# Withdrawing the order between different cells of one PSUM tile in a two-stream recurrence

## The chip, the cores and the metric

The kernel runs on one core of one Trainium2 chip. The metric is the device time of one execution in microseconds (us); the median of three runs stands for a kernel. The profile is of one further execution. Its engines are PE (matmul), DVE (vector), ACT (scalar and tables), POOL (GpSimd) and SP, whose queue issues all the DMAs named here. Each engine takes its own instructions strictly in the order in which the program lists them; between engines, and for data inside an engine, they wait on semaphores.

## What is computed

Two transformer-like layers over x of shape 16 x 512 x 256 (batch, time, channel). Layer 0 has a recurrent "fast weights" block and a low-rank GELU network; layer 1 has attention over a window of 64 with four global keys, and a channel mix. Only the recurrence matters here. For each of 16 x 16 pairs of batch and head it carries two small matrices, `W_in` and `W_out` (4 x 16 each), over 32 chunks of 16 tokens:

```python
def step(carry, xs):
    W_in, W_out = carry
    q_t, k_t, v_t, lr_t = xs
    k_h = softmax(einsum('blhd,bDhd->blhD', k_t, W_in)) * lr_t[..., 1:]
    q_h = softmax(einsum('blhd,bDhd->blhD', q_t, W_in))
    qk = einsum('bqhD,bkhD->bhqk', q_h, k_h) * mask
    o_t = einsum('bqhD,bDhd->bqhd', q_h, W_out) + einsum('bhqk,bkhd->bqhd', qk, v_t)
    W_out = W_out + einsum('bnhD,bnhd->bDhd', k_h, v_t)
    for _ in range(2):
        g_out = -attn(W_in, k_t, v_t)
        g_in = -attn(W_out, v_t, k_t)
        W_in = W_in - lr_in * g_in
        W_out = W_out - lr_out * g_out
    return (W_in, W_out), o_t
```

`attn` is a softmax of scores over the 16 tokens, times values. Every step needs the matrices of the one before it, so within one batch and head nothing of two chunks can run at once.

## The kernel before

The batch is cut into two halves of 8 (8 batches x 16 heads = 128 partitions), the time into 8 blocks of 64. A unit `u` is one half (`u % 2`) and one block (`u // 2`): 16 units. Each passes through five streams: `prepare` (projections, convolutions, loads and stores through DRAM), `chain` (the recurrence), `mlp` (output projection of the recurrence, low-rank network), `attend` (window attention) and `mix`. A timetable by hand gives each step of each stream a due time, and the steps are written down in that order. `chain(u)` lasts from u to u + 2, so at any time two chains run, one of each half: unit u in its first piece of 32 tokens and unit u - 1 in its second. A piece has two chunks. A chunk of unit 9 is called 9_0_1 below: unit, piece, chunk.

From the written order a scheduler makes the order on each engine: it takes instructions by their place in the written order, as their dependencies allow, on its own idea of durations.

The matrices and the small sums of both halves lie in one PSUM tile of one bank, `fw` (128 x 512, lines 493 to 508): the left 256 columns are the first half's, the right 256 the second's. `fast(half)` cuts out `w_in`, `w_out`, `w_outs` and the places of maxima and sums. Every instruction that reads or writes `fw` is DVE's. The framework orders any two uses of one PSUM tile of which one writes, whether or not they touch the same columns; so all the uses of `fw`, of both halves, stand on DVE in the order in which they were written.

One chunk, `recur` (line 585 on), by its lines:

- ACT copies k, q and v of the chunk into `tok` (L597). DVE multiplies `tok` by `w_in` and reduces (scores, L527 and L528): `sc_k`, `sc_q` into `scs`.
- `exp_tokens`: maximum (L539) and difference (L541) on DVE, exponential on ACT (L542, `e_k`). Then `hid` by L609, L612 and ACT's L613.
- `over_tokens` on DVE (L547, L548, L549: sum, reciprocal, scaling), then POOL's outer product `pd_o` (L534); L619 to L623 normalise `hid`, then POOL's `pd_kv` (L534).
- DVE adds `w_out` to `pd_kv` (L628), scans it (L631), copies its end to `fw` (L632), reduces `pd_o` (L636, `do`) and adds (L641).
- Scores of v (`sc_v`, `sv`), exponential `e_v`, `over_tokens` again, POOL's `pd_i` twice (L534); DVE reduces each (L636, `di`) and adds it to `w_in` (L649, L653).
- Scores `sk`, `e_k` again, POOL's second `pd_o`; its reduction and the addition to `w_out` (L657) are put off into the next chunk.
- POOL makes the output from the scan (L661 to L663) into the place of q.

At the end of a piece `finish_piece` normalises the output (L673 to L681; `ov` is L678 and L679) and stores it (L682); `load_piece` loads the next piece (L567, L569), for which the same buffers must be free, and normalises k and q (`ss_k`, `ss_q`: ACT's squares L558, DVE's sums L579, POOL's products L581). `finish_fast_weights` loads the output in another layout, `oT` (L693).

In `attend`, row pair r (0 to 3) of a unit finds its maxima (`sc` by PE, `mx` by DVE in L889 and L900, split by POOL in L215 and L217), then weighs (`pmx`, `st`, `py`, `pz` by PE; `pT` L926 and `rs` L978, L979 by ACT; `yT` L983 by DVE). Its keys are loaded by L790 into a buffer that the unit before has read.

The end of the kernel's main function runs the timetable:

```python
    for _, _, last, stream in sorted(steps, key=lambda s: s[:2]):
        next(stream, None)
        if last:
            assert next(stream, steps) is steps
```

Of the kernel before, what the change touches and what calls it, by code (L numbers as in the profile page):

```python
# [15 lines left out]
PSUM = bass.MemoryType.PSUM  # L16

P = 128
# [50 lines left out]
def parity_scales():  # L69

    ch = np.arange(P)
    even = (ch // D) % 2 == 0
    s = 1.0 / math.sqrt(D)
    group, slot = ch // 32, ch % 32
    part = slot // NS < NPART
    sel = -((slot[:, None] % NS == np.arange(NS)[None, :]) & part[:, None]).astype(np.float32)
    k2, pair, _ = np.unravel_index(np.arange(32), (2, 4, NGLOB))  # L80
    selg = np.stack(
        [(group[:, None] == pair) & (slot[:, None] % NS == 2 * k2 + e) & part[:, None] for e in range(2)], 1
    ).astype(np.float32)
    ones_g = np.tile(np.arange(8)[None, :] == (4 * k2 + pair)[:, None], (NR, 1))
    parts = [
        np.stack([even * s, ~even * s, even, ~even], 1),
        group[:, None] == np.arange(4)[None, :],
        sel,
        -selg.reshape(P, -1),
        ones_g,  # L90
    ]
    return np.ascontiguousarray(np.concatenate([p.astype(np.float32) for p in parts], 1))


@with_exitstack
def adaln_blocks(ctx: ExitStack, tc: tile.TileContext, a: dict, out: bass.AP):
# [11 lines left out]
    def ctile(shape, name):  # L108
        return const.tile(shape, F32, tag=name, name=name)
# [36 lines left out]
    for n in ("cq", "ck", "cv"):  # L146
        t = ctile([P, 2, 4], f"w_{n}")
# [345 lines left out]
    fw = ps_w.tile([P, 512], F32, tag="fw", name="fw")  # L493
# [637 lines left out]
    steps = []  # L1131
# [5 lines left out]
    for _, _, last, stream in sorted(steps, key=lambda s: s[:2]):  # L1137
        next(stream, None)
        if last:
            assert next(stream, steps) is steps  # L1140


# [52 lines left out]
```

## Time and profile before

| what | value |
|---|---|
| three runs | 3187.85, 3193.95, 3194.49 us; median 3193.95 us |
| span of the profiled execution, first to last instruction | 3186.8 us |
| mean granted clock of TensorE | 0.830 |
| first chunk of unit 0 begins | 118 us |
| first chunks of units 1, 4, 8, 12, 15 begin | 229, 704, 1403, 2136, 2679 us |
| last addition to `w_out` (L657) | 2876 us |
| `pwo` of the last unit begins (PE, output projection of its recurrence) | 2958 us |

The time of the profiled execution itself is not among the runs' times; its span lies 1.1 us under the fastest of them and 7.2 us under the median. A unit takes 171 to 177 us while units 4 to 7 begin, and 178 to 186 us from unit 8 to unit 13: attention over more than one block begins to cost there. Idle time is given per instruction with what ended it ("releaser").

### The profile page before, as it was taken

The page shows a single profiled execution, that of the slowest core. Times are in us where ns is not written, and L with a number is a line of the kernel's source. Part 1 is how long each engine was busy: PE and PEld are TensorE (multiplying, and loading weights), DVE is VectorE, ACT ScalarE, POOL GpSimd, SP SyncE. Part 2 cuts the span into 40 slices and gives each one's busy share as a digit, 9 for nine tenths or more (in the row PEclk, how much of TensorE's full clock was granted, in tenths as well). Part 3 has the DMA queues.
Part 4 walks back from the last instruction along what each step waited for, and adds up shares of the span by engine and source line. Part 5 has one row for each costly group of instructions (what it writes and reads, how often), then busy time and mean ns, then how long its engine had stood idle before and what let it go on. Part 6 is the DMA issues. An engine that isn't in the chain of part 4 may idle for free.

```text
span 3186.8 us, 47321 instructions
## 1 busy us (share of the span) xinstructions
PE 2368.4 (74%) x17232; PEld 1450.8 (46%) x17232; DVE 2392.2 (75%) x4513; ACT 1809.4 (57%) x3880; POOL 1588.0 (50%) x1447
## 2 busy tenths in 40 slices
PE   3540255868787887878787787878878788789996
PEld 2210123444444454555545455555545555455564
DVE  1678787878787887888887888888888878875221
ACT  1761364656666756566665656666565655455653
POOL 0245555556556555545546454554645465654111
PEclk7775686878797988879888888988888888889998
DMA  5420122132314131232304123230402312122011
GB/s 150 98 58 13 47 44 62 31 74 54 84 35 100 30 92 44 64 71 51 84 21 104 31 64 71 51 84 23 106 21 66 70 48 60 44 54 59 13 35 27
DMA packets 439307, 186.46 MB, mean 59 GB/s; under 512 B 323937, under 2 KB 413090, under 8 KB 439074
## 3 DMA queue, kind: packets, MB, share of 16 engines
q1 hardware_dynamic: 439074, 183.44, 23.6%
q8 instruction: 135, 2.21, 0.3%
q14 instruction: 98, 0.80, 0.1%
HBM read 116.66 MB, written 66.72 MB: 58 GB/s over the span
## 4 chain that ended last, share of the span: by engine, by line
DVE 36%; PE 21%; POOL 18%; ACT 12%; issue 8%; DMA 4%; SPq 1%; POOLq 0%; DVEq 0%; ACTq 0%
POOL pd_o L534 5%; DVE pd_kv L631 5%; POOL pd_i L534 4%; DVE sc_v L527 4%; DVE sv L528 3%; POOL pd_kv L534 3%; PE pproj L1005 2%; DVE do L636 2%; DVE di L636 2%; DVE mx L889 2%; DVE scs L528 2%; DVE sc_k L527 2%; PE ph L736 1%; DMA oT<-o 1%; POOL x L389 1%
## 5 line engine op out<-in xcount | busy, mean ns | idle before, releaser
L534 POOL TENSOR_TENSOR pd_o<-e_k,dt_v 128x1024 f32<-128x1024 f32 x128 | 299.4, 2347 | 206.8 <-DVE e_k L549 206.6
L534 POOL TENSOR_TENSOR pd_i<-e_v,dt_k 128x1024 f32<-128x1024 f32 x128 | 297.1, 2358 | 54.5 <-DVE e_v L549 54.5
L708 PE MATMUL pwo<-w_WoT,oT 128*128 128x256 f32 x256 | 106.3, 574 | 230.1 <-POOL oT L701 191.0
L873 PE MATMUL st<-qs,keys 32*128 32x128 f32 x2048 | 195.3, 329 | 75.4 <-DVE mx L889 37.2
L636 DVE TENSOR_REDUCE do<-pd_o 128x64 f32<-128x1024 f32 x126 | 152.5, 1214 | 123.2 <-POOL pd_o L534 123.2
L661 POOL TENSOR_TENSOR pd_kv<-hid,pd_kv 128x1024 f32<-128x1024 f32 x64 | 150.0, 2344 | 170.6 <-DVE fw L632 154.2
L873 PE MATMUL sc<-keys,qs 32*128 32x128 f32 x2048 | 183.4, 320 | 62.3 <-DVE mx L889 48.5
L873 PEld LDWEIGHTS st<-qs,keys 32*128 32x128 f32 x2048 | 165.7, 221 | 120.4 <-DVE mx L889 45.7
L636 DVE TENSOR_REDUCE di<-pd_i 128x64 f32<-128x1024 f32 x128 | 155.0, 1215 | 86.0 <-POOL pd_i L534 85.9
L873 PEld LDWEIGHTS sc<-keys,qs 32*128 32x128 f32 x2048 | 146.8, 210 | 129.1 <-DVE mx L889 68.1
L534 POOL TENSOR_TENSOR pd_kv<-hid,dt_v 128x1024 f32<-128x1024 f32 x64 | 151.6, 2368 | 84.2 <-DVE hid L623 76.4
L889 DVE TENSOR_REDUCE mx<-sc 128x4 f32<-128x512 f32 x256 | 168.9, 680 | 31.4 <-PE sc L870 31.3
L631 DVE TENSOR_TENSOR_SCAN pd_kv<-within,pd_kv 128x1024 f32<-128x1024 bf16 x64 | 186.4, 2912 | 0.8
L708 PEld LDWEIGHTS pwo<-w_WoT,oT 128*128 128x128 f32 x256 | 68.4, 287 | 258.3 <-POOL oT L701 205.7
L527 DVE TENSOR_TENSOR sc_k<-tok,fw 128x1024 f32<-128x1024 f32 x128 | 155.6, 1216 | 16.1 <-ACT tok L597 14.5
L926 ACT ACTIVATE pT<-st 128x512 f32<-128x512 f32 x256 | 134.3, 603 | 55.3 <-PE st L870 55.1
L224 ACT ACT_TABLE_LOAD x115 | 147.5, 1283 | 15.9 <-PE ph L736 10.0
L527 DVE TENSOR_TENSOR sc_v<-tok,fw 128x1024 f32<-128x1024 f32 x128 | 150.4, 1215 | 1.6
L528 DVE TENSOR_REDUCE sv<-sc_v 128x64 f32<-128x1024 f32 x128 | 149.6, 1209 | 0.0
L736 PE MATMUL ph<-PT,w_v 64*128 64x512 f32 x256 | 111.3, 685 | 36.1 <-ACT z L224 27.5
L1005 PE MATMUL pproj<-w_proj,yT 128*128 128x256 f32 x512 | 124.4, 387 | 11.5 <-DVE yT L983 9.7
L197 PE MATMUL pmx<-w_w_attnT,blocks 128*128 128x384 f32 x256 | 111.6, 563 | 7.9 <-DVE up_a L387 3.1
(251 smaller groups left out, 6730.5 us busy)
## 6 DMA issues: line engine op xcount, KB each, us to landing
values<-values SPq DMA_DIRECT2D x56, 256.0 KB
gate_a<-gates SPq DMA_DIRECT2D x64, 128.0 KB
xa<-in_x_dram SPq DMA_DIRECT2D x32, 256.0 KB
x<-in_x_dram SPq DMA_DIRECT2D x32, 256.0 KB
gate_c<-gates SPq DMA_DIRECT2D x64, 128.0 KB
gate_d<-gates SPq DMA_DIRECT2D x64, 128.0 KB
q<-y SPq DMA_DIRECT2D x64, 128.0 KB
dt_q<-q SPq DMA_DIRECT2D x32, 256.0 KB
```

The costliest lines, as they stand in the source:

```text
L224: ins = nc.scalar.activation(*args[0], **args[1])
L527: engine.tensor_tensor(pr, tok.unsqueeze(1).to_broadcast(every), w.unsqueeze(2).to_broadcast(every), mul)
L528: nc.vector.tensor_reduce(dst, pr, AX.X, add)
L534: engine.tensor_tensor(pr, hid.unsqueeze(2).to_broadcast(every), tok.unsqueeze(1).to_broadcast(every), mul)
L631: nc.vector.tensor_tensor_scan(flat, within, flat, 0.0, mul, add)
L636: nc.vector.tensor_reduce(t, pr, AX.X, add)
L661: nc.gpsimd.tensor_tensor(po, qh.unsqueeze(2).to_broadcast([P, R, D, CH]), upto, mul)
L708: nc.tensor.matmul(po[:, n * C : (n + 1) * C], lhsT=pair(oT, k, 2 * b2 + n), rhs=w_o[:, k, :], start=k == 0, stop=k == 1,)
L736: nc.tensor.matmul(ph, lhsT=w_v1[rows, f // 2, :], rhs=pT[rows], start=True, stop=True)
L873: nc.tensor.matmul(dst, lhsT=lhsT, rhs=rhs, start=start, stop=False, skip_group_check=True)
L889: nc.vector.tensor_reduce(mx[:, j], sc[j].rearrange("p (s k) -> p s k", s=NS), AX.X, ALU.max)
L1005: nc.tensor.matmul(po[:, n * C : (n + 1) * C], lhsT=yT[:, k2, par].rearrange("p e t -> p (e t)"), rhs=w_proj[:, k2, par, :], start=k2 == 0 ...
```

## The change

The instructions and their data are the same. After the timetable has run, and before the scheduler starts, a new class goes through all the recorded instructions and works out, for every access to every tile, which partitions and which columns it touches (`touched`). From that it gets, for each instruction, the earlier ones that share a cell with it and must stay ahead (`after`). For the tile `fw`, `loosen` adds these as explicit dependencies and declares that all others among the users of `fw` need not be kept. `lines` is empty here, so `ahead` is too.

```diff
+class Timetable:
+    def read(self):
+        self.steps, self.users, self.tile = [], {}, {}
+        seen = {}
+        for ins in self.bb.instructions:
...
+            k, s = len(self.steps), Step(ins)
+            self.steps.append(s)
+            for x, writes in [(x, False) for x in ins.ins] + [(x, True) for x in ins.outs]:
...
+                t = x.bass_ap.tensor
+                (p0, p1), cells = touched(x)
+                if x.bass_ap.space == PSUM and t.tag_meta.bufs > 1:
+                    p0, p1 = 0, P
+                    cells[:] = True
+                writers, readers = seen.setdefault(t.name, ([], []))
+                for group in (writers, readers) if writes else (writers,):
+                    keep = []
+                    for e in group:
+                        j, q0, q1, other = e
+                        if j != k and q0 < p1 and p0 < q1 and (other & cells).any():
+                            s.after.add(j)
...
+                        keep.append(e)
+                    group[:] = keep
+                (writers if writes else readers).append((k, p0, p1, cells))
...
+    def loosen(self, name):
+        users = set(self.users[name])
+        ahead = {k: j for line in self.lines.values() for j, k in zip(line, line[1:])}
+        for k in self.users[name]:
+            s = self.steps[k]
+            for j in s.after & users:
+                self.edge(s.ins, self.steps[j].ins, mybir.DependencyClass.Sync, "cells")
+            keep = [self.steps[j].ins for j in (s.after | {ahead.get(k)}) & users]
+            self.tc.declare_no_dep(
+                s.ins, group=name, keep=keep, query=mybir.DependencyQuery.ANY, reason="other cells"
+            )
+            self.tc.add_to_no_dep_group(name, s.ins)
@@ at the end of the main function @@
         next(stream, None)
         if last:
             assert next(stream, steps) is steps
+    order = Timetable(tc)
+    order.read()
+    order.loosen(fw.name)
```

Line numbers in this text are those of the kernel before; in the changed one the same lines stand 91 further down.

More of the change, by code (lines that the diff above doesn't have):

```diff
@@ L92, in parity_scales, with __init__, touched @@
     return np.ascontiguousarray(np.concatenate([p.astype(np.float32) for p in parts], 1))
+ENGINES = ("PE", "DVE", "Activation", "Pool", "SP")
+class Step:
+    def __init__(self, ins):
+        self.ins = ins
+        self.kind = type(ins).__name__
+        self.engine = str(ins.engine).split(".")[1]
+        self.after, self.tiles = set(), []
+def touched(x):
+    shape = tuple(x.bass_ap.tensor.shape)
+    steps, at, row = [tuple(s) for s in x.ap], int(x.bass_ap.offset), int(np.prod(shape[1:]))
+    if x.bass_ap.space == bass.MemoryType.DRAM:
+        parts, row = (0, 1), int(np.prod(shape))
+    else:
+        step, n = steps.pop(0)
+        parts = (at // row, at // row + (n - 1) * (step // row) + 1)
+        at %= row
+    cells = np.zeros(row, bool)
+    idx = np.array([at])
+    for step, n in steps:
+        if step and n > 1:
+            idx = (idx[:, None] + step * np.arange(n)[None, :]).ravel()
+    cells[idx] = True
+    return parts, cells
@@ new lines, with __init__, edge @@
+class Timetable:
+    def __init__(self, tc):
+        self.tc, self.bb = tc, tc.nc.cur_bb.bb
+        self.lines = {}
+    def read(self):
+        self.steps, self.users, self.tile = [], {}, {}
+        seen = {}
+        for ins in self.bb.instructions:
+            if str(ins.engine).split(".")[1] not in ENGINES or type(ins).__name__ == "BassTilePoolBoundary":
+                continue
+            k, s = len(self.steps), Step(ins)
+            self.steps.append(s)
+            for x, writes in [(x, False) for x in ins.ins] + [(x, True) for x in ins.outs]:
+                if not hasattr(x, "ap") or not hasattr(x.bass_ap.tensor, "tag"):
+                    continue
+                t = x.bass_ap.tensor
[10 more added lines that the diff above has]
+                            s.after.add(j)
+                            if writes and p0 <= q0 and q1 <= p1 and not (other & ~cells).any():
+                                continue
+                        keep.append(e)
+                    group[:] = keep
+                (writers if writes else readers).append((k, p0, p1, cells))
+                self.tile[t.name] = t
+                users = self.users.setdefault(t.name, [])
+                if users[-1:] != [k]:
+                    users.append(k)
+                    s.tiles.append(t.name)
+    def loosen(self, name):
[10 more added lines that the diff above has]
+            self.tc.add_to_no_dep_group(name, s.ins)
+    def edge(self, ins, other, how, reason):
+        self.tc.add_manual_dep(
+            ins, other.name, mybir.DependencyInfo(how, mybir.DependencyReason.DATA), reason=reason
+        )
```

## The prediction

> **What bounds the kernel now.** I read the page's shares first, then the chain that ended last, then the 40 slices.
>
> ```profile
> PE 2368.4 (74%) x17232; PEld 1450.8 (46%) x17232; DVE 2392.2 (75%) x4513; ACT 1809.4 (57%) x3880; POOL 1588.0 (50%) x1447
> DVE 36%; PE 21%; POOL 18%; ACT 12%; issue 8%; DMA 4%; SPq 1%; POOLq 0%; DVEq 0%; ACTq 0%
> PE   3540255868787887878787787878878788789996
> DVE  1678787878787887888887888888888878875221
> ```
>
> No engine is full. In the middle the chain runs through DVE and, between its instructions, through POOL, ACT and PE. The last three slices belong to PE: after `pwo` of unit 15 (2958 us) it is busy 197.3 of 229 us, and its order there is the same in both programs. So a gain must come from the middle. There the view by windows says, for one unit and for a stretch of another kind inside it:
>
> ```profile
> 1766.00:1952.00 186.00, 156.12 (x1144) 96.05 (x1143) 153.94 (x283) 114.63 (x245) 97.24 (x90) 0.84 0.25 61
> 1827.00:1856.00 29.00, 27.56 (x111) 13.94 (x111) 22.93 (x48) 22.20 (x39) 9.16 (x6) 0.88 0.07 21
> ```
>
> Columns: length, busy time of PE, PEld, DVE, ACT, POOL (with instructions), granted clock, DMA share, GB/s. PE and DVE are about level (156 and 154 of 186 us), and in stretches like the second PE alone sets the pace. DVE's idle time, by its releasers, is mostly POOL's outer products:
>
> ```profile
> DVE do L636 <- POOL pd_o L534: 123.2, 67, 4.8
> DVE di L636 <- POOL pd_i L534: 85.9, 51, 4.5
> DVE pd_kv L628 <- POOL pd_kv L534: 21.4, 14, 2.4
> ```
>
> (idle us, instructions, largest). Together 231 us.
>
> **The change, part by part.** Nothing is computed anew: 4,513 DVE, 11,464 matmul and 1,450 POOL instructions stay. Laid side by side, the two built programs differ in order everywhere: on DVE only 1,726 of 4,515 entries lie in common runs, on SP 807 of 1,046. Users of `fw` of one half may now stand between those of the other. The edges inside a half stay, so the recurrence of a half is no shorter by itself.
>
> *A: DVE's gaps.* The timeline shows two kinds of neighbours:
>
> ```profile
> 1810.39 0.29 DVE L547 TENSOR_REDUCE fw<-e_v 128x8 f32<-128x128 f32 x1
> 1810.72 0.22 DVE L548 RECIPROCAL fw<-fw 128x8 f32<-128x8 f32 x1
> 1810.97 0.35 DVE L549 SCALAR_TENSOR_TENSOR e_v<-e_v,lr,fw 128x128 f32<-128x128 f32 x1
> ...
> 1773.76 0.21 DVE L547 TENSOR_REDUCE fw<-e_k 128x4 f32<-128x64 f32 x1
> 1773.88 0.18 DVE L348 BATCH_NORM_AGGREGATE mv_b<-st_b 128x2 f32<-128x6 f32 x1
> 1773.98 0.23 DVE L620 TENSOR_REDUCE qs<-hid 128x16 f32<-128x64 f32 x1
> ```
>
> (start, duration.) An instruction that waits for the one directly ahead starts after its end (median 34 ns over 774 such; 73 more wait for another engine too); one that waits for none or for an older one starts inside its neighbour (median 83 ns before the end, 2,196 cases). A pair of neighbours that depend costs 34 + 83 = 117 ns. The order before has 847 such pairs, the order after 170, as the scheduler now puts instructions of the other half between them. 677 x 0.117 = 79 us of DVE less: 33 before unit 7, 46 after. Bounds: 79, and 33 if PE sets the pace in all later units. I take **-79**, since DVE leads the chain.
>
> The Trainium skill speaks against this term: "VectorE: DVE Perf Modes", section "The DRAIN you can't avoid", says that the next operation starts only when the pipe is empty and that waits between operations cost nothing extra. By it this term would be 0 and my sum 79 us higher; the starts inside the neighbour above contradict it.
>
> *B: waits for POOL's products.* One unit's recurrence waits look so:
>
> ```profile
> 1777.78 1.22 DVE L636 TENSOR_REDUCE do<-pd_o 128x64 f32<-128x1024 f32 x1 [1.37 <-POOL pd_o L534]
> ...
> 1786.00 1.22 DVE L636 TENSOR_REDUCE do<-pd_o 128x64 f32<-128x1024 f32 x1 [1.36 <-POOL pd_o L534]
> ```
>
> I walked unit 9 through both orders, adding rows' durations of the DVE work that stands between a product's request and its use, against POOL's 2.36 per product and what stands ahead of it. First pair of chunks: stalls of 6.6 us before, 1.6 after (all covered but one `di`, third of four products: 7.1 against 5.3 of cover), -5.0. Second pair: 8.3 before, 11.5 after, as POOL takes `x` (1.27) and `dt_q` (2 x 1.52) ahead of products, +3.2. Net -1.8 a unit, ten units: **-18**. A cruder count of missing cover over all products gives 360 before, 372 after; with observed over counted (231/360) that is +8. Bounds -50 (ten units without the second pair's loss) and +32 (ten with that loss alone).
>
> *C: the boundary of a piece, units 1 to 6.* From the last `ov` (L679) to the next piece's `ss_q` (L579) lie the output's product, its store, the load of q and its square: DVE must have other work that long. It had 5.2 us of such work and the passage took 9.7 to 11.6; after the change 6.4 to 12.2 us stand there. The shares of stall that vanish add up, unit by unit, to 1.2 + 6.4 + 3.1 + 5.1 + 5.3 + 5.9 = **-27**; bounds -27 and 0.
>
> *D: the boundary, units 7 to 13, and SP's queue.* Here the cover falls from 11.4 to 8.4 us against a passage of 17.5: +3. And a DMA moves. Before, SP's rows at a boundary are
>
> ```profile
> 2107.69 1.56 SPq L682 DMA_DIRECT2D o<-dt_q  x2
> 2113.23 0.86 SPq L567 DMA_DIRECT2D dt_q<-q  x1
> 2115.16 0.46 SPq L567 DMA_DIRECT2D dt_q<-q  x1
> ```
>
> both stores together, then both loads. After, the load of attention's `keys` (L790) stands between the two stores. It waits until PE has read the old keys (`st` of row pair 3 of unit u-3). `mx` of that row pair (which `st` follows) ends 14 us of DVE work ahead of `ov`, not 50 as before. In the rows `st` ends 12.5 to 23 us after `mx`; the store is ready some 17 us after it. So the store of one half, and behind it the loads of q of both, wait 0 to 6 us; I take 3. **+6** a unit, seven units: **+42**; bounds 0 and 16 a unit (3 + 6 + another 7, should `mx` itself stand later by half of the 14).
>
> *E: attention's last row pair.* From `mx` (L900) to `yT` (L983) of r = 3, DVE had 39 us of other work (46 real; `rs` ready 1 to 5 us early); now 23, and between `yT` of r = 2 and r = 3 stand 10 us while PE needed 15.1. 0 to 5 a unit, 2.5 x 7 = **+18**. The other row pairs keep 30 us or more.
>
> *F: two readers of SBUF.* DVE rows that take two SBUF inputs and start inside a POOL row last until that one ends:
>
> ```profile
> 1771.79 0.18 DVE L900 TENSOR_TENSOR mx<-mx,mg 128x16 f32<-128x16 f32 x1
> 1802.68 2.32 POOL L661 TENSOR_TENSOR pd_kv<-hid,pd_kv 128x1024 f32<-128x1024 f32 x1 [5.63 <-DVE fw L632]
> 1802.78 2.27 DVE L900 TENSOR_TENSOR mx<-mx,mg 128x16 f32<-128x16 f32 x1
> ```
>
> 86 rows lost 117 us. By the orders' overlap (230 us before, 261 after; observed share 117/230) I add **+15**; bounds -10 and +30.
>
> *G: at nothing.* ACT's table loads fall from 236 to 205: 31 x 1.283 = 40 us, covered since ACT idles 43%; uncovered, 17 of them stood directly ahead of an exponential DVE waits for, -22.
>
> Sum: -79 - 18 - 27 + 42 + 18 + 15 = **-49**. The profiled execution's span of 3186.8 becomes 3138; with the 7.2 us by which the median lies above the span, **3145 us**.
>
> **Rivals.**
>
> *R1, the delays of D and E don't come, nor F.* For it: all three are late by few microseconds in my estimate, and everything moves by that much. -79 - 18 - 27 = -124: **3070**.
>
> *R2, slower: SP's queue.* The load of `keys` holds the store and the loads of q of both halves for the full 16 us at each boundary from unit 7, because `st` of row pair 3 comes late: both halves' recurrences stop and DVE with them. 7 x 16 = 112; with A, B, C, E, F: -79 - 18 - 27 + 112 + 18 + 15 = +21, and if E also takes its upper 5 a unit, +38: **3232**. It decides from 91/7 = 13 us a boundary on (79 + 18 + 27 less 18 and 15). Against it: DVE's earlier recurrence would leave PE as it is, and `st` needs only that.
>
> *R3, PE takes the gain.* From unit 7 PE works 150 of 182 us and sets pieces alone, as in the second window. A's 46 us there only lengthen other waits: -49 + 46 = -3: **3191**. Against it: PE still idles a sixth of a unit.
>
> *R4, the change doesn't do what it says.* Then 3194. The built order excludes it: the edges are withdrawn and the order differs, so it gets no chance.
>
> **How the numbers follow.** Forecast 0.47, R1 0.18, R2 0.22, R3 0.13. What a measurement of this kernel can tell from no change is about 0.2%, 6.4 us. Faster takes the forecast, R1 and half of R3 (its 3191 lies inside, and B to F scatter on both sides): 0.47 + 0.18 + 0.06 = 0.71; same 0.07; slower R2, 0.22. The forecast's own range is 3103 (D at 0) to 3185 (A at half). To hold 8 in 10 the range takes in R1 with a little below it (3060), R3, and R2's weaker end (3210, D at 13 a boundary and E at 5): **3060 to 3210**.
>
> **What would show it.** In the profile of the changed kernel: DVE instructions that start after their neighbour's end near 170, not 847, and DVE's busy time as a union down (A); idle ahead of `do`, `di`, `pd_kv` near 220 us (B); `ss_q`'s idle small in units 1 to 6 (C), and in units 7 to 13 about 6 us more, with `st` L870 the last thing the store waited for (D); `yT` waiting on `rs` for r = 3 (E); L900 and L631 longer in the mean (F); 205 table loads (G). The prediction is wrong if a unit from 7 on takes as long or longer while the gaps are gone (R3, R2), or if a wait stands in the chain that none of these parts names.

## The result, and the profile after

| | before | after |
|---|---|---|
| median of four runs, us | 3194.11 (3187.85 to 3194.49) | 3207.75 (3206.30 to 3210.49) |
| ratio to before, 95% interval | | 1.0052 (1.0038 to 1.0067) |
| span of the profiled execution, us | 3186.8 | 3207.1 |
| DVE neighbours that depend on each other | 847 | 170 |
| DVE occupied: busy time as a union, with idle of up to 60 ns between neighbours, us | 2419.3 | 2337.3 |
| DVE idle for longer up to its last instruction, added up, us | 756.2 | 858.5 |
| from DVE's last instruction to the end, us | 11.2 | 11.3 |

The change made the kernel 0.5% slower; 3145 us and a faster kernel had been predicted. Three parts of the page of the changed kernel: busy time, shares of the chain that ended last, and the slices of PE and DVE.

```profile
PE 2331.7 (73%) x17232; PEld 1419.6 (44%) x17232; DVE 2331.1 (73%) x4513; ACT 1768.4 (55%) x3849; POOL 1648.2 (51%) x1447
...
PE   3541154777758586787878888787878897889996
...
DVE  1678787887777877879697877879696878864221
...
DVE 34%; PE 23%; POOL 16%; ACT 13%; issue 9%; DMA 3%; SPq 1%; POOLq 0%; DVEq 0%; ACTq 0%
```

DVE is busy 61 us less, and its gaps under 60 ns fell by 21 us more: term A had promised 79, and 82 are there. But its longer waits grew by 102, and 102 - 82 is the 20 us by which the span grew. The view of DVE's waits shows who released them (idle us in total, times, longest). Line numbers from here on are those of the changed kernel, unless a row of another one is shown.

```profile
DVE yT L1074 <- ACT rs L1070: 126.3, 28, 14.8
...
DVE pp L551 <- ACT pp L548: 67.5, 24, 5.0
...
DVE pd_kv L719 <- POOL pd_kv L625: 60.7, 39, 2.7
DVE fw L638 <- ACT e_k L633: 58.4, 24, 4.7
DVE ov L769 <- ACT osq L649: 49.7, 27, 6.0
DVE do L727 <- POOL pd_o L625: 40.2, 28, 2.5
...
DVE ss_q L670 <- ACT sq_q L649: 27.0, 13, 4.8
```

Before, the same groups had 85.6, 29.0, 21.4, 5.3, 11.6, 123.2 and 28.6; those that the prediction doesn't show:

```profile
DVE yT L983 <- ACT rs L979: 85.6, 23, 13.2
...
DVE pp L460 <- ACT pp L457: 29.0, 22, 3.3
DVE ss_q L579 <- ACT sq_q L558: 28.6, 9, 4.3
...
DVE ov L678 <- ACT osq L558: 11.6, 24, 1.5
...
DVE fw L547 <- ACT e_k L542: 5.3, 7, 2.7
```

So 83 us of waits for POOL's `pd_o` went, and 38 to 53 us each came at `pd_kv` and at four groups that wait for ACT (`yT`, `pp`, the sum of `e_k`, `ov`). ACT itself is busy 41 us less; where its results come later in the places shown below, other work stands ahead of them in its queue.

The loss is not spread evenly. The first chunk of unit 4 starts 15 us earlier than before, that of unit 5 is 5 late, of unit 6 22, of unit 7 29 and of unit 9 30 late; then the delay shrinks, to 12 at unit 14 and 0 at unit 15, and the end is 20 late. From the first `yT` of one unit to that of the next, units 1 to 3 take 187, 187, 186 us (before 171, 171, 179), units 8 to 10 take 181.1 in the mean (before 184.0). (These are attention's units, which run about three units behind the recurrence: the first `yT` of unit 1 stands at 711 us before, the first chunk of unit 4 at 704.) There are three stretches: a loss of 13 us a unit early, a gain of 2 to 8 a unit in units 5 to 10, a loss of some 20 us in the tail.

The windows of the early stretch show the two pairs of chunks (first of unit 5 with second of unit 4, and the pair behind it). Columns as in the view by windows above. Before:

```profile
875.30:949.80 74.50, 63.80 (x397) 34.63 (x395) 63.75 (x128) 51.77 (x107) 42.52 (x34) 0.93 0.09 29
949.80:1046.00 96.20, 70.41 (x468) 46.18 (x467) 75.41 (x149) 58.45 (x132) 56.99 (x56) 0.77 0.40 95
```

After:

```profile
880.50:940.20 59.70, 27.18 (x183) 17.07 (x184) 54.34 (x102) 24.15 (x63) 35.55 (x24) 0.63 0.06 19
940.20:1068.00 127.80, 108.11 (x681) 63.49 (x679) 88.17 (x175) 83.28 (x174) 65.51 (x67) 0.86 0.35 81
```

PE's 864 to 865 matmuls of the two windows are the same in number. Before they are shared 397 to 468, after 183 to 681. The recurrence runs its first pair in 59.7 us instead of 74.5, with fewer instructions of other streams beside it (ACT 63 for 107, DVE 102 for 128). PE has less than half a window of work there (27 of 60 us) and does the rest in the second pair, which now takes 127.8 us instead of 96.2. The pair of pairs takes 187.5 instead of 170.7.

### The profile page after: what moved, and what is told of

The parts are those of the page before. It is cut to its first block, busy times and chain, and to the rows that moved or that the text cites. A ratio compares the mean times of both kernels' runs of the same rounds, so it can differ in the third digit from the quotient of the medians.

```text
span 3207.1 us, 47301 instructions
## 1 busy us (share of the span) xinstructions
PE 2331.7 (73%) x17232; PEld 1419.6 (44%) x17232; DVE 2331.1 (73%) x4513; ACT 1768.4 (55%) x3849; POOL 1648.2 (51%) x1447
## 4 chain that ended last, share of the span: by engine, by line
DVE 34%; PE 23%; POOL 16%; ACT 13%; issue 9%; DMA 3%; SPq 1%; POOLq 0%; DVEq 0%; ACTq 0%
POOL pd_i L625 4%; POOL pd_kv L625 3%; DVE pd_kv L722 3%; DVE sc_v L618 3%; DVE sv L619 3%; DVE mx L980 3%; DVE di L727 2%; PE st L964 2%; DVE mix L1124 2%; POOL pd_o L625 2%; DVE sc_k L618 2%; PE pka L1133 2%; DVE pp L551 2%; PE pp L532 2%; POOL x L480 1%
## 5 line engine op out<-in xcount | busy, mean ns | idle before, releaser
L964 PE MATMUL st<-qs,keys 32*128 32x128 f32 x2048 | 186.0, 331 | 75.0 <-DVE mx L980 40.5
L964 PE MATMUL sc<-keys,qs 32*128 32x128 f32 x2048 | 160.3, 316 | 81.3 <-DVE yT L1074 40.5
L964 PEld LDWEIGHTS st<-qs,keys 32*128 32x128 f32 x2048 | 150.7, 219 | 130.3 <-DVE mx L980 60.5
L722 DVE TENSOR_TENSOR_SCAN pd_kv<-within,pd_kv 128x1024 f32<-128x1024 bf16 x64 | 188.1, 2941 | 0.2
L964 PEld LDWEIGHTS sc<-keys,qs 32*128 32x128 f32 x2048 | 127.7, 205 | 132.1 <-DVE yT L1074 43.5
L545 ACT COPY xp<-pp 128x512 f32<-128x512 f32 x96 | 56.5, 588 | 200.0 <-PE pp L532 188.1
L452 PE MATMUL pt_b<-blocks,xn_b 128*128 128x128 f32 x128 | 32.4, 366 | 177.5 <-ACT xn_b L450 177.5
L633 ACT ACTIVATE e_v<-e_v 128x128 f32<-128x128 f32 x64 | 19.7, 308 | 255.9 <-DVE e_v L632 252.1
L452 PE MATMUL pt_a<-blocks,xn_a 128*128 128x128 f32 x128 | 32.3, 380 | 155.9 <-ACT xn_a L450 154.5
L1074 DVE TENSOR_TENSOR yT<-py,rs 128x256 f32<-128x256 f32 x128 | 48.5, 417 | 128.9 <-ACT rs L1070 126.3
L1096 PE MATMUL pproj<-w_proj,yT 128*128 128x256 f32 x512 | 138.5, 425 | 3.2 <-DVE yT L1074 2.8
```

The costliest lines, as they stand in the source:

```text
L452: nc.tensor.transpose(pt[:, (2 * n + k) * P : (2 * n + k + 1) * P], xn[:, k * P : (k + 1) * P], ident)
L722: nc.vector.tensor_tensor_scan(flat, within, flat, 0.0, mul, add)
L964: nc.tensor.matmul(dst, lhsT=lhsT, rhs=rhs, start=start, stop=False, skip_group_check=True)
L1096: nc.tensor.matmul(po[:, n * C : (n + 1) * C], lhsT=yT[:, k2, par].rearrange("p e t -> p (e t)"), rhs=w_proj[:, k2, par, :], start=k2 == 0 ...
```

## Experiments

**Where the loss sits.** The withdrawal can be limited to some users of `fw`, by the due time that the timetable gave to the step that wrote them down:

```diff
-    order.loosen(fw.name)
+    order.loosen(fw.name, lambda s: 8 <= s.due < 15)
```

That is `mid`; `early` has `s.due < 8`, `end` has `s.due >= 15`. In all three the scheduler orders the whole kernel anew.

> The order is withdrawn only among users of fw written between due times 8 and 15; the earlier and later ones keep the written order. Theory P (three places): the starts of the chunks in the two traces say that the change loses 45 us between units 4 and 7 (from 15 ahead to 30 behind), gains 30 us from unit 9 to the start of unit 15, and loses 20 us behind it. So this kernel keeps the gain alone: 3194 - 30 = about 3164 (3155 to 3175). Rival Q (PE takes the gain everywhere, what is seen in the starts is only the slack between streams): within 6 us of 3194.

> The order is withdrawn only among users of fw written before due time 8. Theory P: the first loss alone, 30 us behind at unit 8 with the order of before from there on: about 3222 (3210 to 3235). Rival Q: within 6 us of 3194.

> The order is withdrawn only among users of fw written from due time 15 on (unit 15 and the second piece of unit 14). Theory P: the last loss alone, 14 us in the chunks of the last piece and 5 behind them: about 3213 (3205 to 3218). Rival Q: within 6 us of 3194.

Measured: `mid` 3170.57 us, 0.9934 of before (0.9917 to 0.9951); `early` 3288.87, 1.0303 (1.0287 to 1.0319); `end` 3210.23, 1.0056 (1.0035 to 1.0076); before beside them 3194.22. So the middle gains 24 us and the end loses 16, each about as the theory of places said. The early part loses 95 where 28 had been expected, and the three add up to +87, not to the +14 of the whole change. With the constraints from unit 8 on as they were, units 8 to 10 of `early` take 190.8 us each, against 184.0 before; the longest waits in each are at `ss_q` (7.9 us), `yT` (5.7) and `pp` (4.1). The same dependencies, entered from another order, settle in another repeating order.

`halves` withdraws only what lies between the halves and keeps the written order inside each:

```diff
-            keep = [self.steps[j].ins for j in (s.after | {ahead.get(k)}) & users]
+            line = s.half
+            j = last.get(line)
+            last[line] = k
+            keep = [self.steps[i].ins for i in (s.after & users) | ({j} if line is not None and j is not None else set())]
```

`s.half` is the half whose columns the instruction uses, so `j` is the user of the same half written last.

> The order is withdrawn only between the halves; inside a half the written order of all users of fw is kept. Theory H (the last loss comes from uses of one half's own cells overtaking each other, since in the last piece only one half runs): the 14 to 20 us of the end come back, and the time is 3187 to 3195. Rival (other streams' DVE instructions, which wait for PE, are put between the links of the recurrence, whichever cells are free): 3203 to 3213, as with the whole change.

Measured 3212.17, 1.0061 (1.0042 to 1.0079): the loss comes also without any move inside a half. It doesn't come in the same places, though: units 1 to 3 take 193.9 us in the mean here (after 186.7), and units 8 to 10 only 176.4 (after 181.1).

Two combinations of the regions, `s.due < 3 or 8 <= s.due < 15` (`mid_and_first`) and `s.due < 15` (`until_15`):

> The order is withdrawn among users of fw due before 3 and from 8 to 15, and kept elsewhere. Theory P (the places add up): the kernel with 8 to 15 alone measured 3170.6; the chunks of unit 3 begin 3 to 21 us earlier when the order is withdrawn from the start, and unit 4 still 15 us earlier, so 3155 to 3163. Rival (an order that comes earlier at unit 3 settles into another cycle afterwards, as it did when the order was withdrawn before 8 alone, 3288.9): 3180 or more.

> The order is withdrawn among all users of fw due before 15, and kept from there on. Theory B (the last loss is made in unit 15: its recurrence overtakes the attention of unit 13 in DVE's queue, and PE's work, put off, must be done in the last piece, where PE is busy 119 of 129 us): the 16 us that the order withdrawn from 15 on cost come back, 3208 - 16 = 3192 (3186 to 3197). Rival (the last loss is work of the other streams left over from earlier units; at the start of unit 15 the changed kernel has 4,252 matmul records to go, against 4,147): 3203 to 3210.

`mid_and_first` 3166.67, 0.9923 (0.9908 to 0.9938), slightly above its expected range; faster than both kernels. `until_15` 3197.97, 1.0029 (1.0018 to 1.0040), between the two expectations: keeping the order in the tail returns 7 to 10 of the 16 us.

The tail shows more when it is timed by itself, from the start of unit 15 to its `pwo`. That takes 278 us before, and 279 and 276 in the two runs below that hold its order or nearly so (`pinned_before`, `light_before`). In every other run it takes 291 to 302: 298 in the changed kernel, but also 291 in `mid`, where nothing is withdrawn from 15 on and unit 15 starts 31 us early. So the tail lost 13 us or more in every order that the scheduler made anew, with or without a withdrawal there.

**What a wait is worth.** `wait_price` keeps the exact order of the changed kernel on all engines and makes each user of `fw` that stands directly behind an independent user wait for it: 1,243 dependent neighbours instead of 170. `pinned_before` holds the order of before on all engines, with the dependencies withdrawn:

```diff
+    for row in rows:
+        for j, k in zip(row, row[1:]):
+            if (j, k) not in sync:
+                order.edge(by[k], by[j], mybir.DependencyClass.NoSync, "order")
+    for j, k in sync:
+        order.edge(by[k], by[j], mybir.DependencyClass.Sync, "wait")
```

`rows` are an engine's instructions in the wanted order, `sync` the pairs that shall wait (none in `pinned_before`).

> Exactly the order of the changed kernel on every engine, and a semaphore wait on its neighbour for every user of fw that stands directly behind another user on which it doesn't depend: neighbours that wait for each other rise from 170 to 1,243. By the rows 1,073 x 0.117 = 126 us more of DVE. Theory A (DVE's own occupation sets the time, as step A took it): the most of it is seen, 3208 + 90 to 126 = 3298 to 3334. Rival Q (most of DVE's occupation lies beside waits for other engines): under 45 us, 3208 to 3253.

> The order of before is written out for every engine as edges without semaphores, and the dependencies between different cells of fw are withdrawn. PE, ACT, POOL and SP run exactly in the order of before; on DVE only neighbouring users of fw change places (2,706 of 4,513 instructions keep theirs, none moves by more than 28 places). Neighbours on DVE that depend on each other fall from 847 to 364. So it is step A alone: 483 x 0.117 = 57 us less of DVE. Theory A (DVE leads the chain, what it saves comes off the time): 3194 - 57 = 3137, and half of it at least (3165 or less). Rival Q (another engine or the fixed order of ACT and PE takes the gain): within 10 us of 3194.

Busy time by the pages, first `wait_price`:

```profile
PE 2355.2 (72%) x17232; PEld 1435.2 (44%) x17232; DVE 2423.8 (74%) x4513; ACT 1767.8 (54%) x3849; POOL 1633.4 (50%) x1447
```

and `pinned_before`:

```profile
PE 2405.3 (73%) x17232; PEld 1475.1 (45%) x17232; DVE 2319.4 (70%) x4513; ACT 1812.3 (55%) x3880; POOL 1631.0 (49%) x1447
```

`wait_price` took 3282.73 us, 1.0290 (1.0275 to 1.0305). DVE's occupied time rose from 2337.3 to 2461.9, by 125 us for 1,073 added waits, 116 ns each: the 117 ns of term A. DVE's longer idle fell by 47, and the time rose by 75 over the changed kernel: 0.60 of what DVE is occupied reaches the end. It lies between the two theories. By this, A's saving of 79 would be worth about 47 in the time, order being equal: an estimate, since waits were added here to the order after, not taken from the order before.

`pinned_before` took 3300.92, 1.0335 (1.0311 to 1.0359), and both theories missed. Its waits fell too (847 to 364 dependent neighbours, occupied time down by 87 us), yet longer idle rose by 202. PE, ACT and POOL ran in the order of before; on DVE some 1,800 of 4,513 instructions stand at other places, by at most 28. So changed places on DVE alone, with fewer waits, can lose 110 us. This does not support a plain price by the number of waits, and A's saving was not seen by itself in the order before.

**Single waits moved.** The order of the changed kernel is held and a few instructions are moved. The early loss is easiest to see at `yT` of row pair 1 of units 1 to 3 (13.5, 12.6 and 12.7 us), in unit 1 on DVE:

```profile
775.32 0.76 DVE L1074 TENSOR_TENSOR yT<-py,rs 128x256 f32<-128x256 f32 x2 [13.47 <-ACT rs L1070]
775.99 0.22 DVE L638 TENSOR_REDUCE fw<-e_k 128x4 f32<-128x64 f32 x1
...
778.62 0.69 DVE L478 TENSOR_TENSOR up_b<-pv,gate_b 128x512 f32<-128x512 f32 x1 [1.13 <-PE pv L850]
```

and on ACT in the same stretch:

```profile
764.00 1.28 ACT L1069 ACT_TABLE_LOAD   x1
765.29 0.60 ACT L1069 ACTIVATE rs<-pz 128x512 f32<-128x512 f32 x1
765.91 1.28 ACT L315 ACT_TABLE_LOAD   x1
767.20 1.84 ACT L315 ACTIVATE z<-ph,c_b 128x512 f32<-128x512 f32 x3
...
772.48 1.28 ACT L325 ACT_TABLE_LOAD   x1
...
774.66 0.63 ACT L1070 ACTIVATE rs<-rs 128x512 f32<-128x512 f32 x1
...
775.65 0.28 ACT L633 ACTIVATE e_k<-e_k 128x64 f32<-128x64 f32 x1
```

`rs` needs two functions of ACT; between them lie 8.8 us, with the network's `z` and two table loads among others. DVE, behind `yT`, has the sum of `e_k` next, whose exponential stands behind `rs` on ACT, so the recurrence stops too. `act_early` moves `rs`, `e_k` and `hid` up on ACT in units 1 to 3:

```diff
   rs<-pz (L1069)
+  rs<-rs (L1070), e_k (L633), hid (L704)
   table load, z, z, z (L315), ...
-  rs<-rs, e_k, hid
```

> The order of the changed kernel, written out for every engine, with one move: on ACT, in units 1 to 3, the second function of rs (L979) of row pair 1 and the recurrence's exponentials e_k and hid of the chunk that waits there go directly behind the first function of rs (L978), ahead of six GELUs of the low-rank network and eight copies. Theory S (the first loss is made there: yT and the softmax of the recurrence stand behind that block in ACT's queue for 13 us a unit): the wait falls by about 7 us in each of three units, 3208 - 21 = 3187 (3180 to 3196). Rival (the wait is slack, something else sets the 187 us of these units): 3203 to 3210.

Measured 3198.62, 1.0025 (1.0016 to 1.0035) against before at 3190.49: 9 us of the loss, between the two theories. The timeline of `act_early` in unit 1:

```profile
767.51 0.76 DVE L1693 TENSOR_TENSOR yT<-py,rs 128x256 f32<-128x256 f32 x2 [6.01 <-ACT rs L1689]
...
779.83 0.69 DVE L1097 TENSOR_TENSOR up_b<-pv,gate_b 128x512 f32<-128x512 f32 x1 [10.19 <-PE pv L1469]
```

The wait at `yT` fell by 7.5 us and the one at `up_b` rose by 9.1: DVE now meets PE's `pv` at about the time at which the changed kernel met it (779.8 and 778.6 us). `links_first` puts the recurrence's links ahead of this as well: on DVE `up_b` and `st_c` behind the scans (L722), on POOL `x` behind `pd_kv`.

> The order of the changed kernel written out, with the moves of act_early, and besides, in the same three places (units 1 to 3): on DVE up_b of the low-rank network and the st_c behind it, which waited 10.2 us in act_early, go behind the two chunks' reductions and scans (L636, L631); on POOL the addition to x that needs up_b goes behind the other half's pd_kv. Theory S (the first loss is made where ready links of the recurrence stand behind others' work in the in-order queues; act_early only moved the wait on to up_b): the scans end 8 to 10 us earlier in each of three units, 3199 - 27 = 3172 (3165 to 3182). Rival (these streams are at their own pace and the recurrence waits for them in any order): 3192 to 3202.

Measured 3198.45, 1.0027 (1.0017 to 1.0036), before 3190.02: nothing more, as the rival said. Its chunks do run ahead of those of `act_early`, by 4 us at the start of units 7 and 15, but the end does not show it. The next instruction of the mlp stream, behind `pproj`, takes over a part of the wait, which now stands ahead of the second scan:

```profile
782.85 0.69 DVE L1097 TENSOR_TENSOR up_c<-pproj,gate_c 128x512 f32<-128x512 f32 x1 [3.31 <-PE pproj L1715]
```

In the tail of the changed kernel the last chunk's sum of `e_v` (L638) comes 16 us after its difference (L632). On DVE it stands behind `yT` and `up_c`, on ACT its exponential behind `rs` and `z`:

```profile
2907.46 0.29 DVE L632 TENSOR_TENSOR e_v<-sv,fw 128x128 f32<-128x128 f32 x1
2914.53 0.76 DVE L1074 TENSOR_TENSOR yT<-py,rs 128x256 f32<-128x256 f32 x2 [6.78 <-ACT rs L1070]
2923.57 0.69 DVE L478 TENSOR_TENSOR up_c<-pproj,gate_c 128x512 f32<-128x512 f32 x1 [8.28 <-PE pproj L1096]
2924.17 0.28 DVE L638 TENSOR_REDUCE fw<-e_v 128x8 f32<-128x128 f32 x1
```

`tail_early` moves the exponential up on ACT, `yT` and `up_c` behind the scaling on DVE, and `pd_i` ahead of `x` on POOL.

> The order of the changed kernel, written out for every engine, with the last exponential of the recurrence (e_v of 15_1_1) moved ahead of rs13_1 and five GELUs on ACT, yT13_1 and up_c13_0 moved behind its scaling (L549) on DVE, and its product pd_i ahead of one addition to x on POOL. In the changed kernel this link stands still from 2907.5 to 2924.2 us. Theory S (the last loss is made in the same way as the first: a link of the recurrence behind other streams' work in the queues of ACT and DVE): up to 14 us come back, 3208 - 14 = 3194 (3191 to 3200). Rival (the end is bound by PE's remaining work, which what is moved behind feeds): 3203 to 3212.

Measured 3205.08, 1.0047 (1.0030 to 1.0064): 2 to 3 us at most, within the spread of the changed kernel (1.0038 to 1.0067), and inside the rival's range. In its timeline the sum comes 1.4 us after the end of the difference, but `yT` and `up_c` wait as long as ever, now ahead of `di`:

```profile
2902.71 0.30 DVE L1257 TENSOR_REDUCE fw<-e_v 128x8 f32<-128x128 f32 x1 [1.39 <-ACT e_v L1252]
...
2909.72 0.76 DVE L1693 TENSOR_TENSOR yT<-py,rs 128x256 f32<-128x256 f32 x2 [6.08 <-ACT rs L1689]
2920.36 0.69 DVE L1097 TENSOR_TENSOR up_c<-pproj,gate_c 128x512 f32<-128x512 f32 x1 [9.89 <-PE pproj L1715]
```

`mid_act` is `mid_and_first`, held, with the second exponential `e_k` of units 8 to 13 ahead of `pT`, `hTc` and `xn` on ACT.

> The order of mid_and_first written out, with one move on ACT in units 8 to 13: the exponential e_k2 of the second chunk goes ahead of four pT, pg, eight copies and two normalisations, behind which DVE waits 4.7 us for it. Theory S (the recurrence sets the pace there too): 6 x 4.7 = 28 us less than mid_and_first, 3167 - 28 = 3139 (3137 to 3150). Rival Q (PE, 152 us of matmuls in a unit of 181, sets the pace; the wait only moves): 3160 to 3170.

Measured 3164.93, 0.9923 (0.9908 to 0.9938): at most 2 us, where the theory of single stalls had 28. Between 1900 and 2440 us DVE's waits for `e_k` fell from 24.7 to 5.9 us, and those at `ov` rose from 8.1 to 16.2.

`feed` holds the order of the changed kernel and moves the end of the mlp stream's normalisation in units 1 to 4 ahead on DVE and ACT. In the changed kernel it ends 49, 22, 27 and 27 us after its first `st_b` there, against about 7 before (38, 9, 11 and 11 in `feed`), and PE's longest wait in the starved first pair (window 880.5 to 940.2 above) is for it:

```profile
PE pt_b L452 <- ACT xn_b L450: 20.7, 1, 20.7
```

> The order of the changed kernel written out, with one thing moved in the low-rank network of units 1 to 4: the end of its normalisation (the late st_b and mv_b, off_b on DVE behind the first scan of the first pair of chunks instead of behind some 15 more links of the recurrence; rs_b, xn_b, hTb on ACT ahead of the exponential e_v that they stood behind). Theory F (the first loss is PE standing idle for this normalisation, 20.7 us in one wait, whose 37 us of matmuls then crowd into the second pair): units 1 to 4 go back towards 171 us, 3208 - 30 to 48 = 3160 to 3178. Rival (another wait sets these units): 3195 or more.

Measured 3210.10, 1.0061 (1.0042 to 1.0080): nothing. The same window of `feed`, by busy time and by PE's waits:

```profile
880.00:940.00 60.00, 30.15 (x163) 19.36 (x162) 56.46 (x101) 25.46 (x67) 36.92 (x26) 0.57 0.05 14
```

```profile
PE sc L1583 <- DVE yT L1693: 9.0, 1, 9.0
PE pt_a L1071 <- ACT xn_a L1069: 7.5, 1, 7.5
PE st L1583 <- DVE mx L1599: 6.2, 2, 3.1
PE pt_b L1071 <- ACT xn_b L1069: 4.8, 1, 4.8
```

PE's wait for `pt_b` fell from 20.7 to 4.8 us. A new one of 9.0 came at `sc`, that at `st` grew from 3.2 to 6.2, and that at `pt_a` (7.5) stayed; PE is still busy for half of the window only.

**First and second pairs.** The windows above suggest that the harm is done in the first pair of chunks of each unit. `pair1` withdraws for `s.due % 1 < 0.5`, `pair2` for `s.due % 1 >= 0.5`, `no_early_pair1` for `s.due < 15 and (s.due % 1 >= 0.5 or s.due >= 8)`.

> The order is withdrawn only among users of fw of the first chunk of each piece (due times with a fraction under 0.5), in all units. Theory F (the recurrence overtakes what feeds PE in the first pair of chunks, into which that normalisation falls): not faster than before, 3194 to 3230. Rival (the loss is made in the second pair): 3180 or less.

> The order is withdrawn only among users of fw of the second chunk of each piece. Theory F: the gain without the first loss, 3155 to 3185. Rival (the loss is made in the second pair): 3205 or more.

> The order is withdrawn from due 8 to 15 and, before 8, for the second chunk of each piece alone; kept from 15 on. Theory F: the gain of mid (3170.6) and that of early second pairs, 3145 to 3170. Rival: 3180 or more.

Measured beside 3190.06: `pair1` 3305.12, 1.0357 (1.0339 to 1.0375); `pair2` 3191.03, 0.9998 (0.9985 to 1.0012); `no_early_pair1` 3190.72, 1.0006 (0.9995 to 1.0018). So the withdrawal in the first pairs alone costs 115 us, far more than theory F had, and in the second pairs alone nothing. But the gain that it expected of the second pairs did not come either. In the traced execution of `pair2` (3181.6 us; its runs spread from 3180 to 3196) units 8 to 10 take only 177.6 us and unit 15 starts 32 us early; the tail, 300 us from there to `pwo` against 278 before, gives most of this back. Units 1 to 3 take 184.6 us there, so the early loss is not one of the first pairs alone. `no_early_pair1` says the same: it is `mid` with the second pairs before 8 added, and these cost it all of the gain of `mid` (1.0006 against 0.9934). So theory F missed in all three, as in `feed`.

**Less work for PE.** Both orders held, with the second half of some contractions and the last six of eight steps of `pQ` over 32 of the 512 columns (these products are left incomplete; the two runs are for the time alone):

```diff
-                        pp,
+                        pp if k == 0 else pp[:, :32],
...
-                pq[rows], lhsT=w_u2[:, f, :], rhs=zs[f], ...
+                pq[rows] if f < 2 else pq[rows, :32], lhsT=w_u2[:, f, :], rhs=zs[f] if f < 2 else zs[f][:, :32], ...
```

> Exactly the order of before on every engine, with less matmul work: in pp, pq, pk and pka the second half of the contraction, in pQ the last six of eight, are taken over 32 columns instead of 512 (so these products are not complete). 576 matmul records of 0.60 to 0.65 us become some of 0.28 (the rows of short ones): about 200 us less of PE in all, 12.6 of 152 in a unit. Theory B (with work spread evenly PE has slack): 20 to 60 us off, 3130 to 3170. Rival: see light_after.

> Exactly the order of the changed kernel on every engine, with the same matmul work left out. Theory B (its loss is PE's crowded second pair): more comes off than from the order of before, 70 to 130 us, and it ends at least 10 us under light_before. Rival W (the loss is in chains of waits through the queues, whatever PE has to do): as much comes off as from the order of before, and it stays 8 to 20 us above light_before.

Measured beside 3188.9: `light_before` 3169.43, 0.9940 (0.9928 to 0.9953); `light_after` 3168.48, 0.9936 (0.9921 to 0.9951). PE is busy 2264.0 and 2214.7 us, 104 and 117 less: about half of the 200 expected, at a lower mean granted clock (0.796 and 0.792, against 0.830 and 0.818 with the full work). Much the same relief is worth 20 us in the order before and 39 in the order after, and the two end level. Yet units 1 to 3 of `light_after` still take 183.1 us against 174.0 in `light_before`: two thirds of the early loss (9.1 of 13.2 us a unit) stay with a lighter PE, and what is made up is made up later. So the time depends on PE's load more in the order after, but PE's load in the second pairs is not all of the early loss: neither theory holds as it stands.

## Why the prediction was wrong

- **A, the gaps (-79).** The size was right: 847 to 170, and 82 us in the trace. The step that failed is "I take -79, since DVE leads the chain". By `wait_price`, where the order is equal, only 0.60 of DVE's occupied time reaches the end, which makes A about 47 us (an estimate, nearer to the low bound of 33 than to 79); and the order was not equal: 102 us of longer waits came with it. The mean share of a chain that runs through four engines says who is on it, not that a saving comes through. The section of the Trainium skill's page "VectorE: DVE Perf Modes" that I weighed ("The DRAIN you can't avoid") would have made A nothing; its finding that a semaphore between two operations costs nothing extra does not hold in `wait_price`, 125 us for 1,073. The section itself says that a next operation that isn't held starts earlier, which I left out; the starts inside the neighbour agree with that.
- **The missing term.** I walked one unit of the recurrence through both orders, and asked of every wait whether the recurrence had cover. I did not ask what the freed recurrence overtakes. This term stood at nothing, and the trace has 102 us more of DVE's longer waits in its place (38 to 53 each at `yT`, `pp`, `pd_kv`, `ov` and the sum of `e_k`, less 83 at `pd_o`). In the first pair of unit 5 PE has 183 matmuls instead of 397, and late results of other streams (`rs` for `yT`, `pv`) stop DVE's queue, and the recurrence in it. That the one makes the other is not shown: `feed` filled the largest hole in PE's work and gained nothing.
- **B, POOL's products (-18).** `do`, `di` and `pd_kv` together fell from 231 to 182 us, better than I said; the waits for `e_k` just ahead of them (L638) rose from 5 to 58, which is more than the gain.
- **C, boundary of units 1 to 6 (-27).** `ss_q` there fell from 24.0 to 7.3 us, -17: right in kind. But `ov`, where that passage begins, waits 13.7 us at the boundaries of units 4 to 6, against 1.9 before, so at most 5 us are left.
- **D, SP's queue (+42).** The mechanism is not in the trace. The load of keys stands between the stores for well under a microsecond, as here in SP's timeline:

```profile
2303.92 0.32 SPq L773 DMA_DIRECT2D o<-dt_q  x1
2304.55 0.57 SPq L881 DMA_DIRECT2D keys<-keys  x1
2305.20 0.61 SPq L773 DMA_DIRECT2D o<-dt_q  x1
```

  What the boundary from unit 7 on does lose, about 3 us a unit, is at `ov`, which waits for ACT's square of the output.
- **E, `yT` (+18).** The place was wrong. Row pair 3 of units 7 to 13 lost 1.3 us in all (10.9 to 12.2); row pair 1 of units 1 to 3 lost 12 to 13 us each, although I had written that the other row pairs keep 30 us or more. I had measured the cover from the second part of `mx` (L900 before), which these early units don't have.
- **F (+15).** +5: the excess over the rows' usual duration rose from 113.9 to 118.8 us. The sign that I had named came for L631 (2.91 to 2.94 us in the mean) and not for L900 (0.64 to 0.27). **G.** 205 loads as counted, and worth nothing that could be seen.
- **Rivals.** R2 had the sign, by a mechanism that did not occur (D). So it is luck that 3207.75 lies inside the range, whose upper end of 3210 was taken from R2. R3, PE taking the gain, is nearer: the time does depend on PE's load in this order, but with a lighter PE units 1 to 3 keep most of their loss, and the units from 7 on, where R3 put it, are the ones that gained.

Shown: the saving of A in DVE's occupied time, the price of added waits with the order held, and where time is won and lost. Not settled is a single cause of the 13 us a unit early, 187 against 174. Five edits that each took away a long wait of a place gave 9, 0, 3, 2 and 0 us. Each time waits elsewhere grew (at `up_b`, `up_c`, `up_c`, `ov`, and at `sc` and `st`), and none of the three early ones brought units 1 to 3 near the 174 us of before (`act_early` 184.3, `links_first` 183.4, `feed` 186.1). A loop through the queues of DVE, ACT and PE would fit this, but no run isolates it. Open, too, is what makes the tail 13 us or more longer in each order that the scheduler made anew. The best version measured is `mid_and_first` (0.9923; `mid_act`, 2 us less, isn't told from it); the second pairs alone from 8 to 15 were not tried.

## What to carry to other kernels

A false dependency can also act as a pacer between streams that share in-order engines: without it the recurrence ran its first pairs ahead of the others' work, and the kernel was slower, though how the one leads to the other stays open. Withdraw it region by region, and compare the length of each unit, for the sum of the regions need not be the whole (here +87 against +14). When gaps are saved on one of several level engines, count a part of them (0.6 where waits were added here) and then look for the freed instructions' new neighbours: what do they now stand ahead of, and who waits for that?

## What the runs showed of the hardware

- A DVE instruction that waits for the one directly ahead of it costs 117 ns more by its rows, 116 ns by the 1,073 waits added, and 70 ns of time each (75 us / 1,073).
- The granted clock of TensorE was mostly lower where PE had less to do: 0.63 in the starved first pair of unit 5 (PE busy 27 of 60 us) and 0.86 in the crowded second (108 of 128), against 0.93 (64 of 75) and 0.77 (70 of 96) before. `feed`'s window shows 0.57 at 30 of 60, so the order by busy share is not strict. Over the whole execution the mean went from 0.830 to 0.818, and to 0.796 in `light_before`, where PE is busy 104 us less than before.
